# A graph layer's segment sum on one core: two of five edge quads bucketed, eight quads to an accumulation

## The chip, the core and the metric

The kernel runs on one core of a Trainium2 chip. A core has five engines, each with its own queue of instructions worked off in order: TensorE (PE in the profile; PEld is its loading of weights), VectorE (DVE), ScalarE (ACT), GpSimd (POOL) and SyncE (SP), which here only issues transfers. They wait for one another by semaphores. Matmul results land in PSUM, which has eight banks; everything else lives in SBUF, 128 partitions wide. GpSimd issues the indirect transfers, which add rows of SBUF to rows of a tensor in device memory.

The metric is the device time of one execution in microseconds, the lower the better: 2198.53 us before, the median of three runs from 2196.79 to 2199.58.

## What is computed

6250 nodes with 128 features, 200,000 edges sorted by `dst`. `src` is drawn evenly from the nodes.

```python
h = jnp.maximum(_layernorm(x, axis=-1), 0.0)
idx_i, idx_j = src, dst
xw = h @ W_in
W_ij = (shifted_softplus(f_ij @ W_f1 + b_f1) @ W_f2 + b_f2) * f_ij_cutoff
x_ij = xw[idx_j] * W_ij
out = jax.ops.segment_sum(x_ij, idx_i, num_segments=6250)
x = x + shifted_softplus(out @ W_o1 + b_o1) @ W_o2 + b_o2
```

`f_ij` has 20 numbers an edge, `f_ij_cutoff` one. The gather runs along the sorted index, the segment sum along the unsorted one.

## The kernel before

**Quads.** Edges are worked in quads of 512, four chunks of 128; there are 391. One iteration i of a loop written out by hand works on several quads at once, each at another stage: `s1` (the filter network's first layer and its softplus) on quad i, `s2` (second layer, gathered rows, product) on quad i−1, `s3` (sum and scatter) on quads i−2 to i−4. `run(i, point)` inserts, at the points L, D0, D1, A0, A1, DM, PE2, A2, D2 and S of an iteration, work that `at(i, point, fn, ...)` registered before. Since every engine works in order, these points set its order.

**Gather.** `dst` is sorted, so 256 edges touch a window of at most 21 nodes. `s1_oh` compares the edges' places in the window (`rb`, on 64 partitions for each of the two quads of a load) with the partition's number, which gives one-hot columns `oh`; a matmul with the window's 63 rows (three bf16 parts of 21 rows) gives `xg` on PE. `s2_copy` (ACT) multiplies by the edges' cut-off from `cT_sb`, `s2_m` (DVE) by `W`.

**Sum, plain quads.** `s1_eq` (DVE) compares the 128 `src` of a chunk with one another; a matmul with that matrix sums, in a chunk, the rows of equal `src` (`s3_pe`), ACT copies them out (`s3_copy`, tile `s`, five buffers), `s3_idx` and `s3_ji` choose one edge of each `src` to be written and send the others to trash rows, and GpSimd adds them to one of four accumulators in device memory, one indirect transfer a chunk (`scatter`).

**Sum, bucketed quads** (`sorted_quads`, 144 of them from quad 5 on, with gaps 3, 2, 3). No scatter. `rank_group` to `rank_slot` give each edge of eight such quads a slot: 16 groups of 392 nodes with 32 slots each, and 64 overflow slots. `perm_oh` makes one-hots of the slots from `iot` (576 numbers), `part_rem` splits the products exactly into three parts, `permute` moves the rows to their slots by matmuls (four blocks of 128 slots; 386 columns: three parts, then the node's place in its group and the group), and `perm_out` (ACT) copies each block to `mst`, two blocks in one tile. `perm_loc` (DVE) converts the node's place to fp32 in `lo`. After six quads (a round, `RND`) come four unit slots, one for each block: `unit_oh` (DVE) makes node one-hots `so` from `iot` and `lo`, `unit_pe` (PE) adds 6 x 3 x 4 matmuls into four banks (32 slots of a group on 32 rows of the array, tag "B", all four buffers of it), and `unit_evac` (DVE) adds the banks to `accT` in SBUF. Overflow rows of two bucketed quads go together through `over_pe` ... `over_scatter`, one indirect transfer a pair; there `over_dg` (ACT) puts the nodes' numbers on a diagonal and `over_row` (PE) spreads it.

**Around it.** While the loop runs, groups of 256 nodes are normalised and multiplied by `W_in` (`prep_...`, 25 groups, the last near iteration 220), edge attributes are split into bf16 parts (`fb_...`, every eight iterations), and near the end accumulator 0 is added to `accT` (`r0_...`). After the loop comes the output network on 13 groups of 512 nodes. `late_cols` loads all cut-offs but the first 128 columns in iteration 7. Where more than two of certain functions stand at PE2, `full[i]` makes ACT copy the plain quad's sums in the same iteration as its matmuls.

Of the kernel before, what the change touches and what calls it, by code (L numbers as in the profile page):

```python
# [20 lines left out]
P = 128  # L21
SC = 1024
SEG = 512
GRP = 16
CAP = 32
OVC = 64
SLOTS = GRP * CAP + OVC
MP0 = 5
MPGAPS = (3, 2, 3)
MPEND = 4  # L30
RND = 6
RKQ = 8
PW = 386
PREP_GAP = 9
# [4 lines left out]
NR = 3 * WIN  # L39
NACC = 4  # L40
EARLY_N = 256


@with_exitstack
def tile_gnn(ctx: ExitStack, tc: tile.TileContext, x, fB, cT, srcT, srcr, dstr, win_, wf1, wf2, bias, bo1c, wo1,
# [18 lines left out]
    caps = base_caps(NP, NSC)  # L64
    ACC_R = NP + P
    ZR = 10 if ACC_R % 10 == 0 else 1
    K1_END, K2_END, K3_END = 2, 8, 140
    Z2, Z3 = [0,0,1,1,2,2,3,3,4,4], [5+2*j for j in range(10)]
    CE = min(128, EP // P)
    GN = NP // GRP  # L70
    mpq = sorted_quads(NQ)
# [4 lines left out]
    for q in range(NQ):  # L76
        if q not in mpi:
            scat[q + 4] += min(4, NCH - 4 * q)
    for q in mpq[1::2]:
        scat[q + 10] += 1  # L80
# [34 lines left out]
    srcT_sb = cp.tile([P, EP // P], I16, name="srcT_sb")  # L115
    cT_sb = cp.tile([P, EP // P], F32, name="cT_sb")
    wo1_sb = cp.tile([P, P], F32, name="wo1_sb")
    wo2_sb = cp.tile([P, P], F32, name="wo2_sb")
    accT = cp.tile([P, NP], F32, name="accT")
    zero = accT[:, :ACC_R // ZR]  # L120
    iot = cp.tile([P, SLOTS], F16, name="iot")
    tri = cp.tile([P, P], BF16, name="tri")
# [178 lines left out]
    def s1_oh(q):  # L301
        rb = loads[q // 2][2]
        j = q % 2
        oh = wk.tile([P, 512], BF16, tag="oh", name="oh")
        v = slice(j * HB, (j + 1) * HB)
        nc.vector.tensor_scalar(oh[v], rb[v], rowid[v], None, op0=ALU.is_equal)
        st[q]["oh"] = oh

# [37 lines left out]
    def s2_copy(q):  # L346
        xc = wk.tile([P, 4, P], F32, tag="xc", name="xc")
        for c in range(4):
            nc.scalar.mul(xc[:, c, :], st[q]["xg"][:, c, :], cT_sb[:, 4 * q + c:4 * q + c + 1])  # L349
        st[q]["xc"] = xc  # L350
# [73 lines left out]
    def rank_group(r):  # L424
        qs = mpq[RKQ * r:RKQ * r + RKQ]
        nc4 = 4 * len(qs)
        srcf = wk.tile([P, 4 * RKQ], F32, tag="srcf", name="srcf", bufs=1)
        for k, q, d, n in runs(qs):
            o = srcf[:, 4 * k:4 * (k + n)]
            nc.vector.tensor_copy(o if n == 1 else o.rearrange("p (j c) -> p j c", c=4), quad_cols(srcT_sb, q, d, n))  # L430
        srcf = srcf[:, :nc4]
        n = [P, nc4, GRP - 1]
        nc.vector.tensor_tensor(ge[:, :nc4, 1:GRP], srcf.unsqueeze(2).to_broadcast(n),
                                thr.unsqueeze(1).to_broadcast(n), op=ALU.is_ge)
        G = wk.tile([P, 4 * RKQ, GRP], BF16, tag="G", name="G", bufs=1)
        nc.vector.tensor_tensor(G[:, :nc4], ge[:, :nc4, :GRP], ge[:, :nc4, 1:], op=ALU.subtract)
        cnt = wk.tile([P, 4 * RKQ], F32, tag="cnt", name="cnt", bufs=1)
        nc.vector.tensor_reduce(cnt[:, :nc4], ge[:, :nc4, 1:GRP], axis=AX.X, op=ALU.add)
        loc = wk.tile([P, 4 * RKQ], F32, tag="loc", name="loc", bufs=1)
        nc.vector.scalar_tensor_tensor(loc[:, :nc4], cnt[:, :nc4], float(-GN), srcf, op0=ALU.mult, op1=ALU.add)  # L440
        ext = wk.tile([P, 4 * RKQ, 2], BF16, tag="ext", name="ext")
        nc.vector.tensor_scalar(ext[:, :nc4, 0], loc[:, :nc4], float(-GN // 2), None, op0=ALU.add)
        nc.vector.tensor_copy(ext[:, :nc4, 1], cnt[:, :nc4])
        rk[r] = {"G": G[:, :nc4], "cnt": cnt[:, :nc4], "ext": ext, "n": nc4, "qs": qs}
# [82 lines left out]
    def perm_out(q, s):  # L527
        a, b = divmod(s, 2)
        if b == 0:
            mp[q]["ms", a] = wk.tile([P, 2, PW], BF16, tag=f"ms{a}", name="mst", bufs=RND + 2 + 2 * a)  # L530
        nc.scalar.copy(mp[q]["ms", a][:, b], mp[q].pop(("q", s))[:, :PW])  # L531

    def perm_loc(q, a):
        lo = wk.tile([P, 2], F32, tag=f"lo{a}", name="lo", bufs=RND + 2 + 2 * a)
        nc.vector.tensor_scalar(lo, mp[q]["ms", a][:, :, 3 * P], float(GN // 2), None, op0=ALU.add)
        mp[q]["lo", a] = lo

    def over_pe(q):
        h = mpi[q] % 2 * OVC
        t = ps.tile([P, 512], F32, tag="B", name="po", bufs=4)  # L540
        o = t[h:h + OVC]
        for c in range(4):
            w = mp[q]["pm"][:, c, GRP * CAP:]
            pt = high(mp[q]["pt"][:, c:c + 1])[:, 0]
            nc.tensor.matmul(o[:, :P + 2], w, pt[:, 2 * P:PW], start=(c == 0), stop=False)
            nc.tensor.matmul(o[:, :P], w, pt[:, P:2 * P], start=False, stop=False)
            nc.tensor.matmul(o[:, :P], w, pt[:, :P], start=False, stop=(c == 3))
        mp[q]["po"] = t

    def over_out(q):  # L550
        h = mpi[q] % 2 * OVC
        mo = mos[mpi[q] // 2 % 2]
        nc.scalar.copy(mo[h:h + OVC, :P + 2], mp[q].pop("po")[h:h + OVC, :P + 2])

    def over_idx(q):
        mo = mos[mpi[q] // 2 % 2]
        so = sp_.tile([P, 1], F32, tag="ovs", name="ovs", bufs=2)
        nc.vector.scalar_tensor_tensor(so, mo[:, P + 1:P + 2], float(GN), mo[:, P:P + 1], op0=ALU.mult, op1=ALU.add)
        mp[q]["so"] = so

    def over_dg(q):
        dg = wk.tile([P, P], F32, tag="dg", name="dg", bufs=1)
        nc.scalar.mul(dg, idt, mp[q]["so"])
        mp[q]["dg"] = dg
        jd = sp_.tile([P, 2], F32, tag="ojd", name="ojd", bufs=2)
        nc.scalar.activation(jd[:, 0:1], mp[q]["so"], AF.Identity, bias=off)
        mp[q]["jd"] = jd
# [11 lines left out]
    def over_sum(q):  # L579
        t = ps.tile([P, 512], F32, tag="B", name="osum", bufs=4)  # L580
        nc.tensor.matmul(t[:, :P + 3], mp[q]["eq"], mos[mpi[q] // 2 % 2][:, :P + 3], start=True, stop=True)
        mp[q]["sum"] = t

    def over_copy(q):
        s = sp_.tile([P, 132], F32, tag="os", name="os", bufs=2)
        nc.scalar.copy(s[:, :P + 3], mp[q].pop("sum")[:, :P + 3])
        mp[q]["os"] = s

    def over_ji(q):
        s, jd = mp[q]["os"], mp[q]["jd"]  # L590
        nc.vector.scalar_tensor_tensor(jd[:, 1:2], s[:, P + 2:P + 3], wgt2, jd[:, 0:1], op0=ALU.is_lt, op1=ALU.mult)

# [8 lines left out]
    def unit_oh(r, s):  # L601
        for q in mpq[r * RND:(r + 1) * RND]:
            so = wk.tile([P, GN], BF16, tag="so", name="so", bufs=RND)
            nc.vector.tensor_scalar(so, iot[:, :GN], mp[q]["lo", s // 2][:, s % 2:s % 2 + 1], None, op0=ALU.is_equal)  # L604
            mp[q]["oh"] = so
# [3 lines left out]
    def unit_pe(r, s):  # L609
# [5 lines left out]
        for q in qs:  # L615
            for k in range(3):
                for g in range(4):
                    v = slice(g * CAP, (g + 1) * CAP)
                    nc.tensor.matmul(ts[g][:, :GN], mp[q]["ms", s // 2][v, s % 2, k * P:(k + 1) * P], mp[q]["oh"][v],  # L619
                                     start=(q == qs[0] and k == 0), stop=(q == qs[-1] and k == 2))  # L620
# [22 lines left out]
    def load_idx(s, lo, hi, tag, **kw):  # L643
# [4 lines left out]
        idx[s, lo] = (dst_sb, src_i)  # L648

    def src_cols(a, b):  # L650
        t_ = wk.tile([P, b - a], I32, tag="f3", name="srci", bufs=2)
# [11 lines left out]
    with tc.manual_schedule():  # L663
# [5 lines left out]
        for i in range(3):  # L669
            ft_ = cp.tile([P, SC], BF16, name=f"ft{i}")  # L670
            fts.append(ft_)
            nc.gpsimd.memset(ft_[96:P, :], 1.0)
        nc.gpsimd.iota(iot, pattern=[[1, SLOTS]], base=0, channel_multiplier=0, allow_small_or_imprecise_dtypes=True)
        xt_load(0)
# [10 lines left out]
        for b in (0, HB):  # L685
            nc.sync.dma_start(bf[b:b + 3], bias[0:1, :].to_broadcast([3, P]))
        nc.sync.dma_start(cT_sb[:, :CE], cT[:, :CE])
        base_i = cp.tile([HALF, 2, SC // WSEG], I32, name="base_i")
# [71 lines left out]
        for mo_ in mos:  # L760
            nc.vector.tensor_copy(mo_[:, P + 2:P + 3], wgt)
        if NQ > 2:
# [14 lines left out]

        def late_cols():
            nc.sync.dma_start(cT_sb[:, CE:], cT[:, CE:])

        at(1 if spread else 0, "D2", rel_ext, 0, rel0)
        if CE < EP // P:
            at(7, "L", late_cols)
            w = -(-(EP // P - CE) // 2)
            for i, a, b in ((11, CE, CE + w), (13, CE + w, EP // P)):
                at(i, "L", src_cols, a, b)
                at(i + 1, "D2", src_narrow, a, b, nc.vector)

        def half_load(k):
# [114 lines left out]
        for q in mpq:  # L904
# [3 lines left out]
            for s in range(4):  # L908
                at(q + 3 + s // 2, "PE2", permute, q, s)
                at(q + 4 + s // 2, "A0", perm_out, q, s)  # L910
            at(q + 4, "DM", perm_loc, q, 0)
            at(q + 5, "DM", perm_loc, q, 1)
            at(q + 4, "PE2", over_pe, q)
            at(q + 5, "A0", over_out, q)
            if mpi[q] % 2:
                at(q + 5, "DM", over_idx, q)
                at(q + 5, "A2", over_dg, q)
                k = clear(q + 6, units)
# [19 lines left out]
        for i in range(max(NQ + 7, last + 14, r0_end + 2)):  # L938
# [4 lines left out]
            if i < NQ:  # L943
                s1_oh(i)
            if 0 <= i - 1 < NQ:
                s1_eq(i - 1)
            run(i, "D1")
            if 0 <= i - 1 < NQ:
# [348 lines left out]
```

## Time and profile before

| What | us |
|---|---|
| median of three runs | 2198.53 |
| the profiled execution's own time | 2198.7 |
| its span, first to last instruction | 2196.8 |
| busy: PE, DVE, ACT, POOL | 1913.6, 1886.5, 1787.2, 1751.8 |
| first and last of ACT's `s1_exp` in the loop (L292) | 23.1, 2083.7 |
| mean granted clock of PE | 0.962 |

A line of a group names the line of the code, the engine, the operation, what it writes and reads with shapes, and the count; then the busy time of all and the mean of one in ns; then the idle time of the engine just before, and what ended it. A line of a timeline gives the start and the duration first, and in brackets the idle time before it. A line of waits names who waited for whom, the total, how often, and the longest. A window gives busy time and the count of instructions for PE, PEld, DVE, ACT and POOL, then PE's granted clock, the share of the DMA engines and GB/s. The idle time of an engine can be the engine's own overhead, and a busy engine need not be the one that sets the end.

### The profile page before, as it was taken

Reading aid. Unit: us, or ns where it says so; the run is one execution under the profiler, and the core shown is the slowest. Engines: PE = TensorE matmul, PEld = TensorE weight load, DVE = VectorE, ACT = ScalarE, POOL = GpSimd, SP = SyncE. Lnnn points to the kernel's source line nnn. Section 1 sums busy time; section 2 is a strip of 40 time slices with the busy share of each in tenths; the row PEclk is TensorE's granted clock in tenths of the full one; section 3 lists DMA queues with packets and bytes.
Section 4 is the critical chain, followed back from the end, with each engine's and each line's share of the span. In section 5 each row is a group of like instructions: output and inputs, shape, how many; then the busy total and the mean of one; then the engine's idle time right before and its main releaser. Section 6 shows DMA issues by size and latency. Waiting matters only on the chain.

```text
span 2196.8 us, 55656 instructions
## 1 busy us (share of the span) xinstructions
PE 1913.6 (87%) x19201; PEld 1373.2 (63%) x19201; DVE 1886.5 (86%) x5123; ACT 1787.2 (81%) x4749; POOL 1751.8 (80%) x1101
## 2 busy tenths in 40 slices
PE   3779899898989989988988999999999989899946
PEld 2556666666656666666666667666666666666724
DVE  5688999988888988898989999989889889898935
ACT  4688888888879887878888989888889888888814
POOL 2678888888888887878778888888888888888884
PEclk9799999999999999999999999999999999999977
DMA  8977777776767676767677667677767766767638
GB/s 263 248 168 145 132 143 144 141 143 125 148 128 145 132 145 129 144 122 148 131 138 143 134 136 148 124 142 144 143 121 148 136 140 129 142 127 152 129 37 235
DMA packets 396414, 316.96 MB, mean 144 GB/s; under 512 B 91839, under 2 KB 335722, under 8 KB 396130
## 3 DMA queue, kind: packets, MB, share of 16 engines
q1 hardware_dynamic: 242546, 240.57, 37.2%
q0 software_dynamic: 153296, 72.75, 33.9%
q8 instruction: 151, 2.47, 0.5%
q14 instruction: 133, 1.09, 0.2%
q10 hardware_dynamic: 288, 0.07, 0.0%
HBM read 173.32 MB, written 139.90 MB: 143 GB/s over the span
## 4 chain that ended last, share of the span: by engine, by line
DVE 34%; PE 20%; ACT 18%; DMA 10%; POOL 9%; issue 7%; SPq 2%; ACTq 0%; DVEq 0%; POOLq 0%
POOL acc L414 9%; DMA acc<-s,ji 6%; PE pq L523 4%; ACT xc L349 4%; PE W L344 4%; PE pp L366 4%; DVE pt L513 4%; DVE so L604 3%; DVE pm L499 3%; DVE a L321 3%; DVE eq L315 3%; ACT mst L531 3%; DVE accT L630 3%; PE un L619 3%; ACT e L293 2%
## 5 line engine op out<-in xcount | busy, mean ns | idle before, releaser
L414 POOL DMA_INDIRECT acc<-s,ji x987 | 1599.8, 1621 | 375.7 <-issue 237.3
L523 PE MATMUL pq<-pt,pm 128*128 128x386 bf16 x2304 | 461.6, 340 | 32.8 <-ACT s L374 26.1
L344 PE MATMUL W<-w,a 128*128 128x128 f32 x3128 | 467.0, 294 | 0.0
L349 ACT ACTIVATE xc<-xg,cT_sb 128x128 f32<-128x128 f32 x1564 | 447.1, 374 | 18.0 <-PE xg L336 14.4
L344 PEld LDWEIGHTS W<-w,a 128*128 128x128 f32 x3128 | 391.3, 196 | 42.5 <-issue 3.3
L619 PE MATMUL un<-so,mst 32*128 32x392 bf16 x6912 | 337.6, 330 | 40.7 <-DVE pr L463 9.4
L366 PE MATMUL pp<-m,eq 128*128 128x129 f32 x1976 | 282.9, 287 | 83.2 <-DVE accT L630 61.2
L523 PEld LDWEIGHTS <-pm 128*128 128x128 bf16 x2304 | 225.6, 99 | 190.1 <-issue 46.2
L366 PEld LDWEIGHTS pp<-m,eq 128*128 128x128 f32 x1976 | 263.6, 197 | 125.3 <-DVE accT L630 86.9
L619 PEld LDWEIGHTS <-mst 32*128 32x128 bf16 x6912 | 208.8, 94 | 164.2 <-issue 60.2
L321 DVE SCALAR_TENSOR_TENSOR a<-z,e 128x512 f32<-128x512 f32 x391 | 266.4, 681 | 49.3 <-ACT e L298 47.3
L374 ACT COPY s<-pp 128x258 f32<-128x258 f32 x494 | 175.1, 393 | 147.2 <-PE pp L366 90.7
L298 ACT ACTIVATE e<-e,con 128x512 f32<-128x512 f32 x391 | 282.4, 722 | 12.7
L293 ACT ACTIVATE e<-e 128x512 f32<-128x512 f32 x391 | 246.5, 631 | 12.4
L531 ACT CAST mst<-pq 128x386 bf16<-128x386 f32 x576 | 246.6, 479 | 10.2 <-PE pq L523 10.2
L292 ACT ACTIVATE e<-z 128x512 f32<-128x512 f32 x391 | 238.6, 610 | 16.2 <-PE z L287 15.9
L630 DVE TENSOR_TENSOR accT<-un,accT 128x392 f32<-128x392 f32 x368 | 182.0, 554 | 38.9 <-PE un L619 23.2
L513 DVE TENSOR_TENSOR pt<-pt 128x512 f32<-128x512 f32 x288 | 198.3, 689 | 0.0
L354 DVE TENSOR_TENSOR m<-W,xc 128x512 f32<-128x512 f32 x247 | 168.1, 681 | 33.7 <-ACT xc L349 28.2
L499 DVE TENSOR_SCALAR pm<-iot,pos 128x576 bf16<-128x576 f16 x576 | 190.4, 392 | 0.0
L354 DVE TENSOR_TENSOR pt<-W,xc 128x512 f32<-128x512 f32 x144 | 99.1, 688 | 87.8 <-ACT xc L349 77.3
L315 DVE TENSOR_TENSOR eq<-sb,srcT_sb 128x512 f32<-128x512 int16 x247 | 168.3, 682 | 3.1
(156 smaller groups left out, 2768.4 us busy)
## 6 DMA issues: line engine op xcount, KB each, us to landing
sb<-src SPq DMA_DIRECT2D x195, 256.0 KB
ft<-fsd SPq DMA_DIRECT2D x195, 240.0 KB
rb<-reld SPq DMA_DIRECT2D x391, 64.0 KB
fsd<-f SPq DMA_DIRECT2D x49, 480.0 KB
acc<-s,ji POOLq DMA_INDIRECT x987
fb<-in_fB_dram SPq DMA_DIRECT2D x49, 320.0 KB
fsd<-f SPq DMA_DIRECT2D x49, 320.0 KB
wn<-tab SPq DMA_DIRECT2D x782, 15.8 KB
```

The source lines that it names most:

```text
L293: nc.scalar.activation(e, e, AF.Exp, scale=-1.0)
L298: nc.scalar.activation(e, e, AF.Ln, bias=half, scale=0.5)
L321: nc.vector.scalar_tensor_tensor(a, st[q]["z"], 0.0, st[q]["l"], op0=ALU.max, op1=ALU.add)
L344: nc.tensor.matmul(W[:, c, :], st[q]["a"][:, c * P:(c + 1) * P], w2, start=False, stop=(c == 3))
L349: nc.scalar.mul(xc[:, c, :], st[q]["xg"][:, c, :], cT_sb[:, 4 * q + c:4 * q + c + 1])
L354: nc.vector.tensor_tensor(m[:, :, :P], st[q]["W"], st[q]["xc"], op=ALU.mult)
L366: nc.tensor.matmul(pp[:, c, :129], st[q]["eq"][:, k, :], m[:, k, :129], start=True, stop=True)
L414: nc.gpsimd.indirect_dma_start(out=accs[k][:, :], out_offset=bass.IndirectOffsetOnAxis(ap=ji, axis=0), in_=s, in_offset=None, compute_op=A ...
L513: nc.vector.tensor_tensor(pt[:, :, k * P:(k + 1) * P], a, high(a), op=ALU.subtract)
L523: nc.tensor.matmul(t[:, :PW], mp[q]["pm"][:, c, s * P:(s + 1) * P], high(mp[q]["pt"][:, c:c + 1, :PW])[:, 0], start=(c == 0), stop=(c == 3))
L531: nc.scalar.copy(mp[q]["ms", a][:, b], mp[q].pop(("q", s))[:, :PW])
L619: nc.tensor.matmul(ts[g][:, :GN], mp[q]["ms", s // 2][v, s % 2, k * P:(k + 1) * P], mp[q]["oh"][v], start=(q == qs[0] and k == 0), stop=(q ...
```

## The change

Constants: bucketed quads start at quad 8 with gaps 2 and 3, in rounds of 8. Code:

```diff
-MP0 = 5
-MPGAPS = (3, 2, 3)
+MP0 = 8
+MPGAPS = (2, 3)
-RND = 6
+RND = 8
-PW = 386
+PW = 387
+MW = 388
+CQ = 16
...
-    cT_sb = cp.tile([P, EP // P], F32, name="cT_sb")
-    iot = cp.tile([P, SLOTS], F16, name="iot")
+    iotw = cp.tile([P, GN // 2 + SLOTS], F16, name="iot")
+    iot = iotw[:, GN // 2:]
...
     def s1_oh(q):
-        rb = loads[q // 2][2]
-        j = q % 2
-        oh = wk.tile([P, 512], BF16, tag="oh", name="oh")
-        v = slice(j * HB, (j + 1) * HB)
-        nc.vector.tensor_scalar(oh[v], rb[v], rowid[v], None, op0=ALU.is_equal)
-        st[q]["oh"] = oh
+        if q % 2 == 0:
+            rb = loads[q // 2][2]
+            oh = wk.tile([P, 512], BF16, tag="oh", name="oh")
+            v = slice(0, min(2, NQ - q) * HB)
+            nc.vector.tensor_scalar(oh[v], rb[v], rowid[v], None, op0=ALU.is_equal)
+            late["oh"] = oh
+        st[q]["oh"] = late["oh"]
...
-        ext = wk.tile([P, 4 * RKQ, 2], BF16, tag="ext", name="ext")
-        nc.vector.tensor_scalar(ext[:, :nc4, 0], loc[:, :nc4], float(-GN // 2), None, op0=ALU.add)
-        nc.vector.tensor_copy(ext[:, :nc4, 1], cnt[:, :nc4])
+        ext = wk.tile([P, 4 * RKQ, 3], BF16, tag="ext", name="ext")
+        nc.vector.memset(ext[:, :, 0], 0.0)
+        nc.vector.tensor_scalar(ext[:, :nc4, 1], loc[:, :nc4], float(-(GN // 2)), None, op0=ALU.add)
+        nc.vector.tensor_copy(ext[:, :nc4, 2], cnt[:, :nc4])
...
     def perm_out(q, s):
-        a, b = divmod(s, 2)
-        if b == 0:
-            mp[q]["ms", a] = wk.tile([P, 2, PW], BF16, tag=f"ms{a}", name="mst", bufs=RND + 2 + 2 * a)
-        nc.scalar.copy(mp[q]["ms", a][:, b], mp[q].pop(("q", s))[:, :PW])
-
-    def perm_loc(q, a):
-        lo = wk.tile([P, 2], F32, tag=f"lo{a}", name="lo", bufs=RND + 2 + 2 * a)
-        nc.vector.tensor_scalar(lo, mp[q]["ms", a][:, :, 3 * P], float(GN // 2), None, op0=ALU.add)
-        mp[q]["lo", a] = lo
+        mp[q]["ms", s] = wk.tile([P, MW], BF16, tag=f"ms{s}", name="mst", bufs=RND + 2 * s)
+        nc.scalar.copy(mp[q]["ms", s][:, :PW], mp[q].pop(("q", s))[:, :PW])
...
     def unit_oh(r, s):
-            nc.vector.tensor_scalar(so, iot[:, :GN], mp[q]["lo", s // 2][:, s % 2:s % 2 + 1], None, op0=ALU.is_equal)
+            w = mp[q]["ms", s].bitcast(F32)
+            nc.vector.tensor_scalar(so, iotw[:, :GN], w[:, 3 * P // 2:3 * P // 2 + 1], None, op0=ALU.is_equal)
...
+    def c_load(b):
+        n = min(4 * CQ, EP // P - 4 * CQ * b)
+        t_ = ld.tile([P, 4 * CQ], F32, tag="cb", name="cb", bufs=2)
+        nc.sync.dma_start(t_[:, :n], cT[:, 4 * CQ * b:4 * CQ * b + n])
+        late["c", b] = t_
...
-            at(7, "L", late_cols)
+        for b in range(1, -(-NQ // CQ)):
+            at(CQ * b - CQ // 2, "L", c_load, b)
...
-            at(q + 4, "DM", perm_loc, q, 0)
-            at(q + 5, "DM", perm_loc, q, 1)
-            if mpi[q] % 2:
+            if q == mpq[-1] and mpi[q] % 2 == 0:
+                at(q + 4, "D2", over_none, q)
+            if mpi[q] % 2 or q == mpq[-1]:
                 at(q + 5, "DM", over_idx, q)
-                at(q + 5, "A2", over_dg, q)
+                at(q + 6, "A0", over_dg, q)
...
+            run(i, "D1")
             if 0 <= i - 1 < NQ:
                 s1_eq(i - 1)
-            run(i, "D1")
```

The node's place in its group keeps its offset of −196: written to the upper half of an fp32 word whose lower half is an extra column of zeros, it is read there as the fp32 it is, and the iota starts at −196 so that the node one-hots compare with it as it stands. The slot one-hots read the same iota from column 196 on. Other lines follow from this: columns of the overflow rows move by one, small tiles get a third buffer, and `over_none` would clear the second half of a pair if the number of bucketed quads were odd. With the new constants there are 152 bucketed quads in 19 rounds and 239 plain ones. Bucketed quads lie at i mod 5 = 3 and 0, a unit slot at every i mod 5 = 0 from 30 on, the last four at 391 to 397 (before: 392 to 398).

## The prediction

> **What bounds the kernel now.** I read the page's engine line first, then the costliest groups, then windows by stage, then the waits of two stages, then POOL's timeline.
>
> ```profile
> PE 1913.6 (87%) x19201; PEld 1373.2 (63%) x19201; DVE 1886.5 (86%) x5123; ACT 1787.2 (81%) x4749; POOL 1751.8 (80%) x1101
> ...
> L414 POOL DMA_INDIRECT acc<-s,ji x987 | 1599.8, 1621 | 375.7 <-issue 237.3
> ```
>
> Four engines between 80% and 87% look balanced, with POOL last. POOL's timeline says otherwise:
>
> ```profile
> 2133.03 1.54 POOL L414 DMA_INDIRECT acc<-s,ji  x1 [0.31 <-issue]
> 2134.88 1.54 POOL L414 DMA_INDIRECT acc<-s,ji  x1 [0.30 <-issue]
> 2136.72 1.54 POOL L414 DMA_INDIRECT acc<-s,ji  x1 [0.30 <-issue]
> 2138.57 1.54 POOL L414 DMA_INDIRECT acc<-os,oji  x1 [0.31 <-DMA acc<-s,ji]
> 2148.10 1.26 POOL L1075 TENSOR_TENSOR ta_in<-ta_in 128x512 f32<-128x512 f32 x1 [7.98 <-DMA ta_in<-acc]
> ```
>
> Behind every scatter lie 0.30 us that count as idle but cannot be used, so a scatter costs 1.62 + 0.31 = 1.93 us. 987 + 72 = 1059 of them fill 2044 us. The first starts at 48.9 us, the last ends at 2140.1, and the tail of the kernel follows that end with 56.7 us. So the span is 48.9 + 2044 + 56.7 = 2150, plus 47 us in which POOL really waits: about 16 among the first dozen scatters, 31 later.
>
> Where are the 31? The windows, divided by the number of quads in each (76, 101, 60, 97, from the count of L292's 391 instructions):
>
> ```profile
> 200.00:600.00 400.00, 362.13 (x3728) 260.42 (x3726) 359.72 (x1009) 344.85 (x926) 333.70 (x207) 0.97 0.72 140
> 600.00:1150.00 550.00, 488.06 (x4980) 350.62 (x4981) 492.38 (x1391) 463.42 (x1254) 447.47 (x279) 0.98 0.71 137
> 1200.00:1500.00 300.00, 283.74 (x2907) 203.36 (x2908) 273.05 (x725) 264.70 (x705) 251.28 (x155) 0.98 0.71 139
> 1500.00:2000.00 500.00, 457.65 (x4719) 326.77 (x4720) 447.05 (x1189) 429.93 (x1142) 421.00 (x260) 0.99 0.71 137
> ```
>
> A quad takes 950/177 = 5.37 us while node groups are still prepared (to about 1150 us), 5.00 just after, 5.15 from 1500 on. POOL's own need is 21.5 scatters in 8 quads, 5.19 us a quad. So from 1200 to 1500 the other engines run faster than POOL and build up work for it; from 1500 POOL holds them back; from 600 to 1150 they are too slow for it. Following quads from their index (L395) to their first scatter agrees: 22.8 us apart at 203 us, 0.9 to 5.7 between 670 and 1080, about 20 from 1550 on. The waits of the two stages:
>
> ```profile
> ACT s L374 <- PE pp L366: 37.2, 27, 3.1
> PEld pp L366 <- DVE accT L630: 34.9, 21, 3.2
> ...
> PEld L619 <- DVE so L604: 9.4, 15, 1.2
> ```
>
> (600 to 1150: PE waits for VectorE's emptying of the banks, and ACT for PE), against
>
> ```profile
> ACT s L374 <- DMA acc<-s,ji: 21.4, 11, 3.7
> ```
>
> (1500 to 2000: ACT waits for a buffer that a scatter still reads). POOL sets the end, and VectorE's lateness starves it in the first half. PE works 4.80 us a quad in the first stage (wait 0.57) and 4.73 in the third (wait 0.27).
>
> **The change part by part.** The lists run out at 152 bucketed quads instead of 144, 19 rounds of 8 instead of 24 of 6, 239 plain quads instead of 247.
>
> *POOL.* 8 plain quads x 4 scatters go, 4 paired overflow scatters come: −28 x 1.93 = −54 us, on the path that sets the end. New need: 3 x 4 + 1 = 13 scatters in 5 quads, 5.02 us a quad. The longer iota at the start (772 columns for 576; 0.6 us now) has 20 us of slack there.
>
> *VectorE.* The rows that shrink:
>
> ```profile
> L630 DVE TENSOR_TENSOR accT<-un,accT 128x392 f32<-128x392 f32 x368 | 182.0, 554 | 38.9 <-PE un L619 23.2 <-issue 14.5
> L306 DVE TENSOR_SCALAR oh<-rb,con 64x512 bf16<-64x512 bf16 x391 | 141.8, 363 | 8.7 <-DMA rb<-reld 2.4
> L535 DVE TENSOR_SCALAR lo<-mst 128x2 f32<-128x2 bf16 x288 | 72.9, 253 | 15.4 <-ACT mst L531 13.1
> L499 DVE TENSOR_SCALAR pm<-iot,pos 128x576 bf16<-128x576 f16 x576 | 190.4, 392 | 0.0
> ```
>
> Window one-hots: 391 to 196, now on 128 partitions. No row has 512 columns on 128; L604 (392 columns, 331 ns) and L499 (576, 392 ns) enclose it, so 363 stays: −195 x 0.363 = −71. Bank emptying: 384 (368 + 16 first ones) to 304, −80 x 0.554 = −44. L535 goes: −288 x 0.253 = −73. Eight plain quads less (eq 0.682, jf 0.214): −7. Eight bucketed more: 32 x 0.392 + 16 x 0.689 + 8 x 0.189 = +25. Unit one-hots +32 x 0.331 = +11. Four overflow pairs more: +3. One rank group more, 32 short copies more (four runs a group) and 19 memsets: +13. Sum −143 us, −0.37 a quad.
>
> The slot one-hots now read the iota 392 bytes into its tile. No row reads at such an offset, so: from 0 to +228 us (608 x 0.375, if 576 columns ran at eq's 0.682 us for 512). I take 0, because the operand is still contiguous, 2 bytes wide and on an even word. The Trainium skill ("VectorE: DVE Perf Modes", Mode 2×_1P) wants 4-byte alignment for packed reads; 392 is 98 x 4, so it would leave the 0.
>
> *PE.* Plain quads −8 x 1.145 (282.9/247) = −9; permutes +8 x 3.206 (461.6/144) = +26; overflow +8 x 0.89 (12 matmuls from 2066.29 to 2067.18 in the timeline) = +7; unit matmuls 6912 to 7296 at 48.8 ns (337.6/6912) = +19; overflow pairs +4 x 0.87, one rank group 1.3: +5. Sum +48, +0.12 a quad: 4.92 in the first stage, 4.85 later. A unit block grows from 72 to 96 matmuls, 3.1 to 4.1 us in one iteration, but comes 76 times instead of 96.
>
> *ACT.* s −16 x 0.393, ji −8 x 0.295, mst +32 x 0.479 (singly as before; one column more), mo +8 x 0.264, overflow +4 x 1.27: +14 us, +0.04 a quad. Moving the diagonal (dg, ojd: 0.69 us a pair) from the end of iteration q+5 to q+6 keeps its cost and takes away its wait for VectorE, 52 us over 72 pairs. Behind it now stand ji and xc; after a unit block xc waits for PE anyway, so I book nothing; without that cover 76 x 0.69 = 52 us come back. PE's over_row stands in the same iteration behind the matmuls for xg, W, z and pp and is not late.
>
> *Unit one-hots without L535* wait for ACT's copy itself, which stands earlier in the same iteration: nothing. Moving the emptying ahead of eq helps only where the quad before was plain; under the new gaps it never is after a unit slot, so nothing.
>
> *SP.* Cut-offs arrive in 25 loads of 64 columns instead of 2: +23 issues, about 0.35 us each, behind load_sc, 8 quads (40 us) before use, into a buffer last read 8 quads earlier. SP's queue holds 2% of the chain, so nothing; 8 us if SP were the path.
>
> The Trainium skill ("SBUF — State Buffer", Who interferes with whom) says VectorE's two-port and two-SBUF-input instructions lock GpSimd out of a shared port. In the trace undisturbed scatters take 1.54 us and the mean is 1.62, 83 us in all. By the rule, with 12% less such VectorE time, about 10 us would go (an estimate of mine); by the row alone nothing, and I count nothing.
>
> **The sum.** POOL's stream: 48.9 + 1031 x 1.93 + 16 = 2055 if always fed. How long is it starved? VectorE is the engine that loses work, and PE's waits in the first stage named it. I take PE's wait to fall there from 0.57 to the 0.27 of the relaxed stage: 4.92 + 0.27 = 5.19 a quad; and to 0.22 later: 5.07. Then POOL starves 200 x 0.17 − 20 (the work piled up early) = 14, and 186 x 0.05 = 9: 23 us where 31 are now. −54 − 8 = −62: the profiled execution's 2198.7 (span 2196.8 and 1.9 around it; the median of the runs, 2198.5, is the same) becomes **2137**. Never starved: −85, 2114.
>
> **Rivals.**
> 1. *PE takes over, half way.* For: PE grows while it is the busiest engine, up to 95% of the time in the third window. Wait 0.42 and 0.24: 5.34 and 5.09 a quad, starved 64 − 20 + 13 = 57 us, +26 − 54: 2171. Against: its waits name VectorE.
> 2. *The longer unit block starves the others: slower.* During 4.1 us of unit matmuls nothing reaches ACT, and all four banks stay taken; if PE's waits hang on this and not on VectorE's load, they stay 0.57 and 0.27. Then 5.49 and 5.12 a quad, starved 94 − 20 + 19 = 93, +62 − 54 = +8: 2207. It decides from a first-stage pace of 5.45 on. Against: 20 blocks fewer, the diagonal's wait gone.
> 3. *The one-hots lose their rate* at the new offset: VectorE −143 + 228 = +85, 0.22 a quad more, so 5.59 in the first stage and 5.22 later; starved 114 − 20 + 37 = 131, +100 − 54: 2245. Only the offset speaks for it.
> 4. *No change*: the gains fall where POOL was not short and are given back; starved about 85 us, 2198.
>
> **How the numbers follow.** Forecast 0.58 (its own range 2114 to 2155), first rival 0.22, second 0.12, third 0.03, no change 0.05. A measurement of this kernel tells about 0.2% from nothing. Faster 0.82, same 0.04, slower 0.14. The range reaches from POOL always fed, 2114, past the first rival to 2182.
>
> **What would show it.** Right: 1031 scatters, POOL back to back through most of the loop, VectorE near 1745 busy, PE near 1960, PE's waits for accT less than half, a first-stage pace near 5.2. Wrong: accT or "xc <- PE xg" waits grown (second rival), pm above 0.5 us (third), scatters with idle before them that ends on ACT's index (first).

## The result and the profile after

The changed kernel takes 2119.49 us (median, 2118.38 to 2121.6) against 2197.66 of the kernel before: a ratio of 0.9647, interval 0.9631 to 0.9664. The forecast was 2137, its own range 2114 to 2155. (With a fourth run, the median of the kernel before is 2197.66 instead of 2198.53.) The profiled execution spans 2117.0 us against 2196.8.

From the page of the changed kernel, the busy time of the engines and the group of its scatters:

```profile
PE 1915.6 (90%) x19769; PEld 1392.3 (66%) x19769; DVE 1763.7 (83%) x4710; ACT 1789.3 (85%) x4781; POOL 1695.6 (80%) x1073
...
L417 POOL DMA_INDIRECT acc<-s,ji x955 | 1538.3, 1611 | 350.3 <-issue 222.8
```

VectorE's busy time fell by 123 us, POOL's by 56, and PE and ACT are where they were. The windows of the four stretches shown of before (columns as there; L294's counts give 77, 108, 63 and 100 quads):

```profile
200.00:600.00 400.00, 376.26 (x3918) 272.41 (x3917) 351.93 (x976) 354.01 (x961) 330.66 (x205) 0.98 0.74 143
600.00:1150.00 550.00, 519.10 (x5540) 376.46 (x5538) 485.70 (x1343) 494.67 (x1339) 461.79 (x287) 1.00 0.75 145
1200.00:1500.00 300.00, 293.33 (x3132) 215.04 (x3131) 268.70 (x704) 278.31 (x743) 252.24 (x157) 1.00 0.75 142
1500.00:2000.00 500.00, 479.15 (x5078) 349.30 (x5077) 428.13 (x1098) 444.55 (x1189) 415.13 (x260) 0.99 0.75 143
```

From 600 to 1150 POOL now issues 287 scatters where it issued 279: with 0.305 us behind each they fill 549 of the 550 us. In that stretch 108 quads go by instead of 101. POOL's waits for ACT's index there, before and after (total, times, longest):

```profile
POOL acc L414 <- ACT ji L395: 21.4, 12, 6.1
```

```profile
POOL acc L417 <- ACT ji L398: 1.5, 5, 0.3
```

POOL's timeline at the end of the loop (start, duration, what, idle time before it):

```profile
2056.72 1.54 POOL L417 DMA_INDIRECT acc<-s,ji  x1 [0.30 <-issue]
2058.57 1.54 POOL L417 DMA_INDIRECT acc<-os,oji  x1 [0.31 <-issue]
2068.24 1.26 POOL L1081 TENSOR_TENSOR ta_in<-ta_in 128x512 f32<-128x512 f32 x1 [8.12 <-DMA ta_in<-acc]
```

POOL still ends last: its last scatter ends at 2060.1, the loop's last `s1_exp` starts at 2000.4, and the tail behind the stream is 56.9 us as before (56.7). So the whole gain lies in the stream. Adding up all scatters of the two traces:

| POOL's stream | before | after | difference |
|---|---|---|---|
| scatters | 1059 | 1031 | −28 |
| their durations, us | 1716.0 | 1660.0 | −56.0 |
| mean of one, us | 1.620 | 1.610 | |
| 0.305 us behind each | 323 | 314 | −9 |
| other idle time in the stream | 52.6 | 36.7 | −15.9 |
| of it between 100 and 1150 us | 31.5 | 16.0 | −15.5 |
| of it between 600 and 1150 us | 17.7 | 1.0 | −16.8 |
| end of the last scatter | 2140.1 | 2060.1 | −80.0 |

28 scatters at 1.925 us are 54 us, the cheaper scatter gives 10.6, the better feeding 16, nearly all of it between 600 and 1150 us.

### The profile page after: what moved, and what is told of

Its sections match the earlier page's. It is cut to its first block, busy times and chain, and to the rows that moved or that the text cites. A ratio compares the mean times of both kernels' runs of the same rounds, so it can differ in the third digit from the quotient of the medians.

```text
span 2117.0 us, 56533 instructions
## 1 busy us (share of the span) xinstructions
PE 1915.6 (90%) x19769; PEld 1392.3 (66%) x19769; DVE 1763.7 (83%) x4710; ACT 1789.3 (85%) x4781; POOL 1695.6 (80%) x1073
## 4 chain that ended last, share of the span: by engine, by line
PE 32%; ACT 20%; DVE 19%; DMA 10%; POOL 10%; issue 7%; SPq 2%; ACTq 0%; DVEq 0%; POOLq 0%
POOL acc L417 10%; DMA acc<-s,ji 8%; PE un L620 8%; PE W L347 7%; PE pq L527 6%; ACT xc L352 5%; PE pp L369 4%; ACT mst L533 3%; DVE so L605 3%; ACT e L295 3%; ACT e L294 2%; ACT e L300 2%; DVE pm L503 2%; ACT s L377 2%; DVE a L324 1%
## 5 line engine op out<-in xcount | busy, mean ns | idle before, releaser
L417 POOL DMA_INDIRECT acc<-s,ji x955 | 1538.3, 1611 | 350.3 <-issue 222.8
L527 PE MATMUL pq<-pt,pm 128*128 128x387 bf16 x2432 | 484.1, 339 | 26.5 <-ACT s L377 19.2
L352 ACT ACTIVATE xc<-xg,cb 128x128 f32<-128x128 f32 x1564 | 446.4, 374 | 46.9 <-PE xg L339 45.0
L620 PE MATMUL un<-so,mst 32*128 32x392 bf16 x7296 | 355.1, 331 | 41.8 <-DVE pr L467 18.4
L527 PEld LDWEIGHTS <-pm 128*128 128x128 bf16 x2432 | 238.6, 99 | 187.7 <-issue 36.1
L620 PEld LDWEIGHTS <-mst 32*128 32x128 bf16 x7296 | 223.0, 94 | 169.3 <-issue 63.0
L369 PE MATMUL pp<-m,eq 128*128 128x129 f32 x1912 | 261.4, 280 | 17.0 <-DVE accT L631 15.0
L533 ACT CAST mst<-pq 128x387 bf16<-128x387 f32 x608 | 260.4, 480 | 8.3 <-PE pq L527 8.3
L294 ACT ACTIVATE e<-z 128x512 f32<-128x512 f32 x391 | 242.0, 619 | 16.7 <-PE z L289 16.1
L631 DVE TENSOR_TENSOR accT<-un,accT 128x392 f32<-128x392 f32 x288 | 142.5, 556 | 47.3 <-PE un L620 32.1
L289 PE MATMUL z<-ft,ws 123*128 123x512 bf16 x391 | 151.9, 389 | 17.9 <-DMA ft<-fsd 17.9
```

The lines of the kernel that those rows point to most:

```text
L294: nc.scalar.activation(e, st[q]["z"], AF.Abs)
L352: nc.scalar.mul(xc[:, c, :], st[q]["xg"][:, c, :], late["c", q // CQ][:, 4 * (q % CQ) + c:4 * (q % CQ) + c + 1])
L369: nc.tensor.matmul(pp[:, c, :129], st[q]["eq"][:, k, :], m[:, k, :129], start=True, stop=True)
L417: nc.gpsimd.indirect_dma_start(out=accs[k][:, :], out_offset=bass.IndirectOffsetOnAxis(ap=ji, axis=0), in_=s, in_offset=None, compute_op=A ...
L527: nc.tensor.matmul(t[:, :PW], mp[q]["pm"][:, c, s * P:(s + 1) * P], high(mp[q]["pt"][:, c:c + 1, :PW])[:, 0], start=(c == 0), stop=(c == 3))
L533: nc.scalar.copy(mp[q]["ms", s][:, :PW], mp[q].pop(("q", s))[:, :PW])
```

## Experiments

All edits are to the changed kernel unless said otherwise; times are medians, with the ratio to the kernel before on the same chip.

**Which of the two halves, code or lists?**

```diff
-MP0 = 8
-MPGAPS = (2, 3)
-RND = 8
+MP0 = 5
+MPGAPS = (3, 2, 3)
+RND = 6
```

> The changed code with the old lists (144 bucketed quads from quad 5, gaps 3, 2, 3, rounds of 6): one window one-hot for two quads, no conversion of the node's place, the diagonal in the next iteration, cut-offs by blocks; 1059 scatters as before. Theory (GpSimd's stream of scatters sets the end, VectorE's lateness only starves it): the stream keeps its length, starvation falls from 31 us to about 10 and a scatter gets about 0.01 us cheaper, so 2160 to 2175. Rival (VectorE's load sets the pace, since its rows fall by 143 us here as in the full change): 2120 to 2135. Rival (all lies in the lists): 2190 to 2198.

2163.44 us, ratio 0.9842 (0.9825 to 0.9858), inside the theory's range. Its parts are not the theory's: 1059 scatters with a mean of 1.603 us give 19 us (the theory had about 11), and idle time in the stream of 38.0 instead of 52.6 us gives 15 (the theory had 21).

The other half, in the frame of the changed kernel, with the window one-hots of before for each quad and conversions for blocks 0 and 2:

```diff
...
+        v = slice(j * HB, (j + 1) * HB)
+        nc.vector.tensor_scalar(oh[v], rb[v], rowid[v], None, op0=ALU.is_equal)
...
+    def perm_loc(q, s):
+        lo = wk.tile([P, 1], F32, tag=f"lo{s}", name="lo", bufs=RND + 2 * s)
+        nc.vector.tensor_scalar(lo, mp[q]["ms", s][:, 3 * P + 1:3 * P + 2], 0.0, None, op0=ALU.add)
+        mp[q]["lo", s] = lo
...
-                at(q + 6, "A0", over_dg, q)
+                at(q + 5, "A2", over_dg, q)
```

> The new lists (152 bucketed quads, rounds of 8, 1031 scatters) with the old work on VectorE put back: a window one-hot for each quad, two conversions for each bucketed quad (of blocks 0 and 2, read by their unit one-hots), the diagonal at the end of iteration q+5. Theory: the stream is 54 us shorter, but VectorE's load is that of before and PE's 48 us higher, so starvation stays at 30 to 55 us: 2145 to 2170. Rival (VectorE's load sets the pace): 2195 to 2215. Rival (all lies in the lists): 2115 to 2125.

2154.35 us, ratio 0.9814 (0.9797 to 0.983). The halves bring 33 and 42 us (1.6% and 1.9%), together about the whole. VectorE is busy 1862.7 us here, 24 less than before, because the fewer emptyings belong to the lists and the conversions have one element instead of two; the scatter's mean is 1.630 us. Neither "VectorE's load is the time" nor "all lies in the lists" survives.

**How fast are the other engines without POOL?** Both kernels with three scatters of four for a plain quad:

```diff
-            scat[q + 4] += min(4, NCH - 4 * q)
+            scat[q + 4] += min(3, NCH - 4 * q)
...
-        for c in range(nchunks(q)):
+        for c in range(min(3, nchunks(q))):
             scatter(st[q]["s"][:, c, :P], st[q]["ji"][:, c:c + 1])
```

> The changed kernel without the last of four scatters of each plain quad, so a quarter of the plain quads' rows is missing from the sums; GpSimd's stream falls to about 790 scatters (some 1520 us) and cannot be the bound. It shows the pace of the other engines alone. Theory (GpSimd still sets the end of the changed kernel, with 25 us of work piled up at the loop's end): 2040 to 2065. Rival (PE, busy 94 to 98% in the windows, is the bound now): 2105 to 2120.

> The kernel before without the last of four scatters of each plain quad (a quarter of the plain quads' rows is missing from the sums). Theory: the other engines keep 5.35 us a quad in the first stage and 4.95 later and no backlog is left at the end: 2115 to 2145, so that the others alone were about 80 us slower than those of the changed kernel. Rival (GpSimd was not the bound before): 2185 to 2198. Rival (VectorE's relief does nothing for the others' pace): the same as the changed kernel without its last scatters, within 15 us.

2054.36 us (changed) and 2129.52 (before), both inside the theory's ranges. From the page of the changed kernel with three of four:

```profile
L417 POOL DMA_INDIRECT acc<-s,ji x717 | 1201.2, 1675 | 550.6 <-ACT ji L398 315.7
```

Now POOL's idle time ends on ACT's index (315.7 us), so POOL waits for the others. That is how a line looks where POOL is not the bound; in the changed kernel the same column reads "issue", POOL's own 0.3 us. So POOL cost the kernels 65 (after) and 67 us (before) over the others' pace, and the change made the others' pace 75 us faster as well. (Leaving scatters out also takes away their transfers and what they delay on the other engines, so that the others' pace beside the full stream may be a little slower than this.) That explains why a change that moves work from POOL to PE did not turn PE into the bound.

**Parts of the code, one at a time.**

```diff
-        if q % 2 == 0:
...
-            v = slice(0, min(2, NQ - q) * HB)
...
+        j = q % 2
...
+        v = slice(j * HB, (j + 1) * HB)
...
```

> The changed kernel with the window one-hot made for each quad again (391 instead of 196, +71 us of VectorE by the row of before). Theory (the other engines are 65 us faster than GpSimd's stream, so VectorE's load costs only through the scatters it delays): 2119 to 2131. Rival (each part of the code pays its share of the 33 us it brought with the old lists, wherever it stands): 2132 to 2140. Rival (VectorE's time is the kernel's time): 2180 to 2195.

> The changed kernel with two conversions on VectorE put back for each bucketed quad (304 x 0.25 = +77 us; the unit one-hots of blocks 0 and 2 read them). Theory: 2119 to 2131, as for the split one-hots, and both and the diagonal together then cost more (2154) than their sum, because only together do they use up the reserve. Rival (additive shares): 2132 to 2140. Rival (VectorE's time is the kernel's time): 2185 to 2200.

> The changed kernel with the diagonal of the overflow pairs back at the end of iteration q+5, where ACT waits for VectorE (52 us over 72 pairs before). Theory (the wait costs only through delayed scatters, and little work is piled up in the first stage): 2119 to 2130. Rival (additive shares of the code's 33 us): 2129 to 2136. Rival (ACT sets the pace): 2155 to 2175.

Split one-hots 2146.38 us, conversions (one element each) 2126.68, the diagonal back at q+5 2120.74 (ratios 0.977, 0.9683 and 0.964, with intervals 0.9744 to 0.9797, 0.9666 to 0.9699 and 0.9624 to 0.9657). Added up, +27, +7 and +1 are the 35 us between the changed kernel and the lists alone. The conversions here cost VectorE 304 x 0.142 = 43 us by their row and not the 77 of the expectation, which is why they come once more below. My expectation for the one-hots was wrong, no range of it holds 2146, and so was the idea that only all three together use up a reserve: nearly all of the code's share is the one-hot for two quads. In the trace with split one-hots VectorE is busy 80 us more, the scatter's mean is 1.624 us (+14 us in all), and idle time in the stream 53.0 us (+16). The waits between 600 and 1150 us, split one-hots:

```profile
PEld pp L368 <- DVE accT L630: 18.9, 13, 2.9
POOL acc L416 <- ACT ji L397: 18.3, 14, 4.3
PE pp L368 <- DVE accT L630: 16.1, 12, 2.5
```

and changed kernel:

```profile
PEld pp L369 <- DVE accT L631: 13.7, 11, 2.2
...
PE pp L369 <- DVE accT L631: 9.5, 9, 1.8
...
POOL acc L417 <- ACT ji L398: 1.5, 5, 0.3
```

PE waits longer for the emptied banks, and POOL, which the changed kernel keeps fed there, runs dry. That is about half of the cost; the dearer scatter is the other half.

**Is it VectorE's load, or its operands?** An extra, unused product for each quad, once with two SBUF inputs (the first of the two products below), once with one of them in PSUM (the second):

```diff
         st[q]["a"] = a
+        xt = wk.tile([P, P], F32, tag="xt", name="xt", bufs=1)
+        nc.vector.tensor_tensor(xt, idt, onesf, op=ALU.mult)
+        nc.vector.tensor_tensor(xt, st[q]["z"][:, :P], onesf, op=ALU.mult)
```

> The changed kernel with an extra, unused VectorE product of two SBUF tiles (128x128 fp32, about 0.29 us) for each quad, +115 us of VectorE. Theory (such an instruction keeps GpSimd from writing a scatter's descriptors while it runs): a scatter's mean grows from 1.61 to 1.63 to 1.66 us, and with the lateness that this load brings the time is 2155 to 2190, at least 12 above the same load with a PSUM input. Rival (a scatter's price does not depend on VectorE's operands, only VectorE's load counts): both within 6 us of one another.

> The same extra product for each quad, but with one factor read from the bank of z in PSUM, so only one input from SBUF. Theory: a scatter's mean stays at 1.61 within 0.01; only VectorE's load counts, which like the split one-hots (+80 us busy, half of their 27 us by starvation) starves GpSimd in the first stage: 2135 to 2160. Rival: as with two SBUF inputs, within 6 us.

2135.47 us (ratio 0.9712, 0.9696 to 0.9728) and 2126.61 (0.9669, 0.9651 to 0.9687). Both lie under the theory's ranges, and the 9 us between the two lie between what theory and rival expected. The scatter's mean is 1.609 and 1.605 us, so the growth to 1.63 us or more did not come. The 391 instructions of 0.278 us, 109 us in all, raise VectorE's busy time by 75 and 73 us and the idle time in POOL's stream to 49.1 and 48.9. Placed after `s1_guard`, they cost 7 to 16 us, while the one-hots' 71 us (80 busy), at the start of each iteration and ahead of the emptying, cost 27. Load alone does not make the difference.

Part of what does is seen when the scatters of a trace are sorted by what VectorE is doing as they start. The extra is a scatter's duration less 1.542 us, the median after the change; number of scatters and mean extra in ns:

| VectorE as a scatter starts | before | after | split one-hots |
|---|---|---|---|
| nothing | 136, 4 | 165, 2 | 151, 2 |
| `a` (one input in PSUM) | 124, 3 | 132, 1 | 114, 3 |
| `pt<-pt` (two inputs in SBUF) | 100, 253 | 107, 281 | 96, 230 |
| `eq` (two inputs in SBUF) | 71, 174 | 56, 229 | 73, 209 |
| `oh`, the window one-hot | 61, 251 | 20, 25 | 61, 192 |

For scatters that start during `eq` the extra is what is left of `eq` at that moment, less 125 ns, and nothing where less than that is left: so in 70 of 71 scatters before and 55 of 56 after, within 25 ns. GpSimd waits there until VectorE is nearly done. From the timelines (start and duration first) of the changed kernel and of the two with extra products:

```profile
711.50 0.68 DVE L318 TENSOR_TENSOR eq<-sb,srcT_sb 128x512 f32<-128x512 int16 x1
711.57 2.02 POOL L417 DMA_INDIRECT acc<-s,ji  x1 [0.30 <-issue]
```

```profile
2002.28 0.27 DVE L327 TENSOR_TENSOR xt<-idt,onesf 128x128 f32<-128x128 f32 x1
2002.28 1.69 POOL L419 DMA_INDIRECT acc<-s,ji  x1 [0.30 <-issue]
```

```profile
1976.93 0.28 DVE L327 TENSOR_TENSOR xt<-z,onesf 128x128 f32<-128x128 f32 x1
1976.94 1.54 POOL L419 DMA_INDIRECT acc<-s,ji  x1 [0.30 <-issue]
```

34 scatters start during a product of two SBUF tiles, and 7 of them take over 1.6 us; 40 start during a product with a factor in PSUM, and none is more than 2 ns longer. So VectorE's operands do count, as the theory had it, but so short a product delays few scatters and adds 1.0 us in all; the rest of the 9 us is not explained by it. The scatters that start during a window one-hot add 15.3 us before, 11.7 with split one-hots and 0.5 in the changed kernel. Nearly all of it comes where `eq` stands right behind the one-hot (39, 38 and 9 scatters with 14.9, 11.4 and 0.2 us). That makes about 11 of the 27 us of the split one-hots. Why such a pair delays a scatter so much more with the one-hot of one quad than with that of two is not shown.

The conversions once more, with two elements as before the change:

```diff
-        lo = wk.tile([P, 1], F32, tag=f"lo{s}", name="lo", bufs=RND + 2 * s)
-        nc.vector.tensor_scalar(lo, mp[q]["ms", s][:, 3 * P + 1:3 * P + 2], 0.0, None, op0=ALU.add)
+        lo = wk.tile([P, 2], F32, tag=f"lo{s}", name="lo", bufs=RND + 2 * s)
+        nc.vector.tensor_scalar(lo, mp[q]["ms", s][:, 3 * P:3 * P + 2], 0.0, None, op0=ALU.add)
```

> The two conversions of each bucketed quad, but of two elements each instead of one (the column of zeros and the place), as before the change. With one element they took 0.14 us each, all alike, and the time was 2127. Theory (the two-element form shares a port with GpSimd and waits for it, as the 0.17 to 0.49 us of the conversions before suggest): mean 0.20 to 0.27 us with a longest near 0.49, 2126 to 2140. Rival (the spread before came from the wait for ACT's copy): 0.14 us, 2122 to 2130.

2124.66 us (ratio 0.9667, 0.9647 to 0.9687). The instruction in three kernels (shortest, median and longest in ns): before, with one element, with two:

```profile
L535 DVE TENSOR_SCALAR lo<-mst x288: 146/171/493, 85.9 to 2090.1; 128x2 f32<-128x2 bf16 x144
```

```profile
L537 DVE TENSOR_SCALAR lo<-mst x304: 133/142/156, 99.7 to 2008.1; 128x1 f32<-128x1 bf16 x152
```

```profile
L537 DVE TENSOR_SCALAR lo<-mst x304: 148/164/494, 99.4 to 2006.7; 128x2 f32<-128x2 bf16 x152
```

One element never takes more than 156 ns, two up to 494, with means of 142 and 234: the form makes the instruction slower, as the theory had it, not the wait for ACT's copy. It goes with POOL's scatters: two-element conversions that start in the first 0.4 us of a scatter take 0.16 us on average, those that start 0.4 to 1.0 us behind a scatter's start 0.23 to 0.33, and one-element conversions 0.14 wherever they start. The kernel's time is the same with both, within the intervals, and lies in the rival's range, 1 us under the theory's.

**The lists.** Rounds of 8 with the old quads, and a denser list:

```diff
-MP0 = 8
-MPGAPS = (2, 3)
+MP0 = 5
+MPGAPS = (3, 2, 3)
-        mp[q]["ms", s] = wk.tile([P, MW], BF16, tag=f"ms{s}", name="mst", bufs=RND + 2 * s)
+        mp[q]["ms", s] = wk.tile([P, MW], BF16, tag=f"ms{s}", name="mst", bufs=(9, 10, 12, 13)[s])
```

> The changed code with the old quads (144 from quad 5, gaps 3, 2, 3) but rounds of 8: 72 unit blocks of 96 matmuls for 96 of 72, 96 emptyings of banks fewer (-53 us of VectorE) than with rounds of 6, the same 1059 scatters. To be read against the same code with rounds of 6 (2163). Theory (the scatters' number sets the end once GpSimd is fed): 2152 to 2163. Rival (the longer accumulation is what pays in the lists): 2120 to 2140. Rival (the longer block starves the others): above 2170.

2178.02 us, ratio 0.992 (0.99 to 0.9939): 15 us slower than the same code with rounds of 6, although VectorE is busy 38 us less (1729.4). That is the last rival's range, not the theory's. So longer accumulations bring nothing by themselves, and here they cost. The two profiled executions lie only 7 us apart; 1.608 us a scatter for 1.603 and 1.7 us more idle time account for those, and the rest of the 15 is not explained. The buffers for `mst` differ too (13 instead of 14 for the last block, one more for the first), which was not tried alone. What the lists bring is the number of scatters.

```diff
-MPGAPS = (2, 3)
+MPGAPS = (2, 3, 2, 3, 1, 3, 2, 3)
```

> The changed kernel with gaps 2, 3, 2, 3, 1, 3, 2, 3: 160 bucketed quads in 20 rounds, 1003 scatters (54 us of stream less), PE +48 and ACT +14 us, some bucketed quads next to one another. Theory (GpSimd's stream at 2119, the others alone at 2054 and some 40 us later with the new load): the others become the bound, 2085 to 2110. Rival (GpSimd still the only bound): 2062 to 2072. Rival (PE is the bound already, or adjacent quads stall it over the banks): 2120 to 2170.

2131.29 us, ratio 0.9697 (0.967 to 0.9725): 12 us slower than the changed kernel with 28 scatters fewer. The waits of POOL between 600 and 1150 us:

```profile
POOL acc L417 <- issue: 56.4, 185, 0.3
POOL acc L417 <- ACT ji L398: 36.4, 13, 9.2
```

POOL waits 36.4 us there for ACT's index where the changed kernel waits 1.5, so the others have become the bound, but further than the theory said: the time lies in the last rival's range (2120 to 2170), and the idle time in the stream is 91 us for 37. This list also puts bucketed quads next to one another, so load and stalls over the banks are not separated. None of the versions tried that computes the whole sum is faster than the changed kernel.

## Why the prediction was right

*POOL's stream sets the end.* Shown: the tail behind the stream is the same in both kernels, the three terms of the stream add up to the gain, and taking a quarter of the plain scatters away saves 65 to 67 us in either kernel.

*−54 us by count.* The count came as said, 1031 for 1059, and 28 x 1.925 = 54. This is two thirds of the gain.

*Starvation from 31 to 23 us.* The direction and the wait named were right, the size was not. Measured behind the first 100 us it fell from 36 to 22 (52.6 − 16.8 and 36.7 − 14.7), by 14 for 8. (The "first dozen scatters" hold 13 us; 16.8 is the sum of the first 100 us.) PE's wait in the first stage fell to 950/185 − 4.84 = 0.30 us a quad, close to the 0.27 taken. The pace was 5.14 for 5.19 because PE's work was 4.84 for 4.92, and after 1200 us 300/63 = 4.76 for 5.07. At 4.76 the others outrun POOL, which needs 5.02, so the 9 us that the sum has for this stage do not follow. Also, 31 was read from the trace and 23 was worked out from paces: the same working for the kernel before gives 200 x 0.18 − 20 = 16, so it did not by itself yield a fall, and that the −8 had the right sign is in part luck. With the measured paces it gives 4 after, a fall of 12; between 200 and 1150 us the traces show 21.2 and 7.9.

*PE +48 us.* Wrong: +2. This is the step that erred most, and the paces rest on it. The rows of the bucketed quads came as summed (permutes 484.1 for 487, unit matmuls 355.1 for 356), but pp fell by 21.5 instead of 9 and W by 5, with shorter means (280 for 287 ns, 292 for 294). Added up one by one, PE's rows grew by 17 us; the engine's busy time counts overlapping spans once and grew by 2. The granted clock was 0.962 before and 0.971 after; what made the matmuls shorter was not separated. PE's share rose from 87% to 90% only because the span shrank.

*VectorE −143 us.* Measured −123. Added up one by one, VectorE's rows fell by 149, so the rows were priced well and their overlap was left out: the conversions put back in the two-element form sum to 71 us by their row (304 x 0.234) but raise VectorE's busy time by 32 (1795.3), and the kernel's time by 5. The enclosed price of the wide one-hot was right: 368 ns for the 363 taken.

*A scatter's price unchanged.* The mean fell by 10 ns, 10.6 us in all; this and the feeding are what the forecast was too high by. The rule of the Trainium skill ("SBUF — State Buffer", Who interferes with whom) gave about 10 by estimate, the row alone 0. The traces bear out what the rule says of two SBUF inputs, scatter by scatter: one that starts during `eq`, with two SBUF inputs, waits, and one that starts during `a`, with one in PSUM, does not (mean extra 229 and 1 ns after the change). That the size agreed is luck in part, for the estimate spread the gain over all such VectorE time. The scatters that start during a window one-hot account for it by themselves, with 15.3 us of extra before and 0.5 after, while those that start during `pt<-pt` cost more (25.3 and 30.0).

*Diagonal, unit one-hots, cut-offs, iota offset at nothing.* The diagonal's wait fell from 52.0 to 5.4 us, and putting it back costs 1 us, within the noise. The slot one-hots at the new offset take 387 ns for 392, so the third rival is gone. That is in keeping with the alignment that the prediction cites from the Trainium skill ("VectorE: DVE Perf Modes", Mode 2×_1P); no run here has a misaligned operand. The cut-off loads alone were not tried.

*The rivals.* The sign that the second named did come: ACT's xc waits 45.0 us for PE's xg where it waited 14.4. It did not decide here, but with the old quads the longer block cost 15 us. Of the first, that the others take over, the kernel with 160 quads shows something; whether PE's load or stalls over the banks are the cause there is open.

## What to carry to other kernels

An engine at 80% that shows a fixed idle time before every instruction may be full: divide the window by its instructions before ranking engines by busy share. Where such a stream sets the end, price an edit by the instructions that it takes from the stream, by the time that the stream is starved, stage by stage, and by what else is running as each of the stream's instructions starts; here 71 us of VectorE work cost 27 in one place and 109 us cost 7 in another. And a balance is near its end when work moved off the bound engine makes its queue run dry, as eight more bucketed quads did.

## What was not expected of the hardware

- A VectorE conversion of two elements takes 148 to 494 ns, of one element 133 to 156 ns.
- PE's granted clock between 600 and 1150 us rose from 0.98 to 1.00 while PE was busy 519.1 us of it instead of 488.1.
- A scatter that starts while VectorE works on `eq`, which reads two inputs from SBUF, takes longer by what is left of `eq` less 125 ns (55 of 56 scatters of the changed kernel, up to 485 ns); during `a`, with one input in PSUM, the mean extra is 1 ns.
- With a quarter of the plain scatters left out, a scatter got dearer, not cheaper: 1.675 us against 1.611 (row L417). More of them start during `eq` there (82 for 56, with 23.9 us of extra for 12.8), and those that start during a unit one-hot wait longer (37 with 27.6 us for 75 with 4.9).
